# A decoder layer on one core: background work moved between scores and values, key differences that last a whole unit, and the row of maxima turned by VectorE and DRAM

## The chip, the cores and the metric

The kernel runs on 1 core of one Trainium2 chip. The metric is device time in microseconds, the median of several runs; before the change it is 2693.47 us (three runs, 2692.97 to 2693.5). A profile is one execution taken by the hardware profiler, with times in microseconds (us) unless marked ns. Engines are named as in it: PE is TensorE's matmul, PEld its weight load, DVE is VectorE, ACT ScalarE, POOL GpSimd, SP SyncE, which here issues every DMA.

## What is computed

Two sequences of 2048 tokens with 512 features go through one layer, all in float32:

```python
x = x + attn(layernorm(x), W_q, W_k, W_v, W_o)   # 16 heads of 32, rotary positions, full softmax
x = x + xattn(layernorm(x), ctx, ctx)            # gelu(x @ ctx.T) @ ctx, 77 rows of context
x = x + ffn(layernorm(x), weights, scale, bias)  # clip((x @ sign(weights).T) * scale + bias, -100, 100)
```

The softmax of the attention is taken with the maximum subtracted: `exp((q.k - max) / sqrt(32))`, divided by its sum over all 2048 keys.

## The kernel before

**Stages.** For each of the two batches, `project_batch` makes queries, keys and values chunk by chunk (128 tokens each) and keeps them in SBUF: keys and queries transposed, features on partitions, so that the four heads of a group `g` lie on four quarters of 32 partitions. `Attention.run` then does the attention. What follows it for a block of 512 tokens (output projection, the attention on the context, the feed-forward) is the generator `after_attention`, which is put into `queue` and taken piece by piece as *background*. After the second batch a tail does the last block alone.

**Units, steps, halves.** A unit `u` is 256 queries of one group of four heads (32 units a batch). It has 8 steps `i` (`STEPS`), each with two chunks of keys for all four heads, done in two halves of two heads. In `run`, the loop over `heads, others` writes the order of PE, DVE, ACT and POOL by hand (`tc.manual_schedule`): PE gets scores of the two heads (L565), maxima of the other two for a later step (L472), more scores; ACT takes the exponentials (L705), POOL adds the two chunks (L707), DVE reduces the maxima (L484). Then come the values of the *previous* step (`weigh`, L583) and the sums of the step before that (`total`, L597), then background. SP's order is not written out by hand.

**Row of maxima.** Scores are formed with keys on partitions, so the maximum of a query must be subtracted along the free axis. `lower` (L550) does it by a matmul that starts a score bank with the negative maxima, from `mrow`. To get there, `maxima` computes scores with queries on partitions, `AHEAD` steps ahead of their use; `split_maxima` writes each maximum as three bfloat16 parts (POOL) into `mt`; `turn_maxima` turns that by one DMA transposition (L504), for unit 0 by PE (L508).

**Differences of keys.** The four score banks of a unit are not cleared at each step: step `i` adds the product with the *difference* of two key blocks (`dk`, built by `key_steps`), so a bank moves from one block of keys to the next. The steps go through the four key blocks twice, first their first halves, then their second halves. At steps 0 and 4 (`i % NB == 0`) the bank is begun anew: `lower`, and keys instead of differences.

**PSUM.** Score banks `st` are four buffers of pool `ps_t`. The maxima `ps` and, during attention, the outputs of background pieces share the three buffers of `ps_s` in turn, so a maxima matmul waits until DVE has reduced what was in its buffer.

**Background.** Each `yield` of `after_attention` ends a piece and says whether the next one has PE work (`True`: heavy). `background(n, light=True)` runs nothing if the next piece is heavy. A block's heavy pieces are four projections (`po`, L382), four turns kept (`pt`, L345), one product with the context (`ph`, L389), four products back (`po`, L408), and four times a turn (`pt`) and a product of the feed-forward (`pf`, L363): 21 in all. Before, a heavy piece may run behind the second half of any step; in the last four units behind the first half too.

**Division.** A unit's sums and values end in one bank `acc`; in the first steps of the next unit `divide` copies it (ACT L611), takes reciprocals in two parts (DVE L617) and multiplies (POOL L620), one part for each `finish()`. In step 1 of a unit there are no sums due, so `total` issues nothing.

**Lead-in.** The maxima of the first `AHEAD` steps of a batch are computed in `project_batch`: `open_block` makes a step due when its block of keys is complete, `att.lead` issues them between the projections. The last ones, with `split_maxima(0)` and `turn_maxima(0)`, are in an order written by hand at its end (L254 to L274).

Of the kernel before, what the change touches and what calls it, by code (L numbers as in the profile page):

```python
# [16 lines left out]
P = 128  # L17
# [8 lines left out]
HQ = 256  # L26
NU = NB * ND * 2
STEPS = NCH // 2
AHEAD = STEPS + 2
SCALE = 1.0 / math.sqrt(DK)  # L30
EPS = 1e-5
MAX_VAL = 100.0
# [4 lines left out]
def decoder_layer(  # L37
# [48 lines left out]

    x_next = [load_x(0, 0), load_x(0, 1)]
    qkv = load_qkv()
    cos = const.tile([P, NCH, DK // 2], F32, tag="cos", name="cos")
    sin = const.tile([P, NCH, DK // 2], F32, tag="sin", name="sin")  # L90
    nc.sync.dma_start(cos, rope_cos.rearrange("(p c) d -> p c d", p=P))
    nc.sync.dma_start(sin, rope_sin.rearrange("(p c) d -> p c d", p=P))

    ident = const.tile([P, P], F32, tag="ident", name="ident")
    make_identity(nc, ident)
# [7 lines left out]
    nc.scalar.activation(minus_half, ones[:, :CPB], AF.Identity, scale=-0.5)  # L103


    mts = []
    for n in range(2):
        mt = const.tile([P, 2, 4, DK], BF16, tag=f"mt{n}", name=f"mt{n}")
        nc.vector.memset(mt, 0.0)
        mts.append(mt)  # L110

    late = {}

# [63 lines left out]

    def project_batch(b, ahead, att, xnt, wk, wq, wv):  # L180
        def times(dst, xnt, w, part=range(ND)):
            for i in part:
                nc.tensor.matmul(dst, xnt[:, i, :], w[:, i, :], start=(i == 0), stop=(i == ND - 1))  # L183
# [22 lines left out]

        def rotate(ch, a, ps, r):
            half = [P, H, DK // 2]
            cs = cos[:, ch, None, :, None].to_broadcast(half + [2])
            sn = sin[:, ch, None, :].to_broadcast(half)  # L210
# [234 lines left out]
    class Attention:  # L445
# [13 lines left out]
        def maxima(self, n, heads):  # L459
# [25 lines left out]

            return reduce

        def split_maxima(self, u):
            mx = self.mx.pop(u)
            neg = small.tile([P, 2, 4], F32, tag="neg", name="neg")  # L490
            nc.vector.tensor_reduce(neg, mx, AX.X, ALU.max, negate=True)
            mt = mts[u % 2]
            nc.gpsimd.tensor_copy(mt[:, :, :, 0], neg)
            nc.gpsimd.tensor_tensor(neg, neg, mt[:, :, :, 0], ALU.subtract)
            nc.gpsimd.tensor_copy(mt[:, :, :, 1], neg)
            nc.gpsimd.tensor_tensor(neg, neg, mt[:, :, :, 1], ALU.subtract)
            nc.gpsimd.tensor_copy(mt[:, :, :, 2], neg)


        def turn_maxima(self, u):  # L500
            mt = mts[u % 2]
            mrow = small.tile([P, 2, P], BF16, tag="mrow", name="mrow")
            if u > 0:
                nc.sync.dma_start_transpose(mrow, mt.rearrange("p c h d -> p (c h d)"))  # L504
            else:
                pt = ps_s.tile([P, 2, P], BF16, tag="s", name="ptm")
                for c in range(2):
                    nc.tensor.transpose(  # L508
                        pt[:, c, :], mt[:, c].rearrange("p h d -> p (h d)"), ident_b
                    )  # L510
                nc.vector.tensor_copy(mrow, pt)
            self.mrow[u] = mrow.rearrange("p c q -> p (c q)")

        def key_steps(self):
            self.dk = [None] + [
                const.tile([P, ND, BLK], F32, tag=f"w{n}", name=f"dk{n}") for n in "kqv"
            ]

            def differences(g):
# [12 lines left out]
            for _ in differences(0):  # L534
                pass
            queue.append(others())


        @staticmethod
# [19 lines left out]
        def scores(self, u, i, heads, c):  # L559
            qb, g, hf = self.units[u]  # L560
            kb, kc = divmod(self.chunk(i, c), CPB)
            keys = self.dk[kb] if kb else self.k[kb]
            for h in heads:
                r = self.rows[h]
                nc.tensor.matmul(  # L565
                    self.st[h][:, c, :],
                    keys[r, g, kc * P : (kc + 1) * P],
                    self.q[qb][r, g, hf * HQ : (hf + 1) * HQ],
                    start=False,
                    stop=True,  # L570
                    skip_group_check=True,
                )
# [74 lines left out]
        def run(self):  # L647
# [37 lines left out]
            for t in range(NU * STEPS):  # L685
# [10 lines left out]
                pw = big.tile([P, 4, 2, HQ], F32, tag="s", name="pw")  # L696
                sm = sums.tile([P, 4, HQ], F32, tag="sm", name="sm")
                for heads, others in (((0, 1), (2, 3)), ((2, 3), (0, 1))):
                    if i % NB == 0:
                        self.lower(u, heads)  # L700
                    self.scores(u, i, heads, 0)
                    reduce = self.maxima(t + AHEAD, others)
                    self.scores(u, i, heads, 1)
                    for h in heads:
                        nc.scalar.activation(pw[:, h], self.st[h], AF.Exp, scale=SCALE)  # L705
                    hs = slice(heads[0], heads[1] + 1)
                    nc.gpsimd.tensor_add(sm[:, hs, :], pw[:, hs, 0, :], pw[:, hs, 1, :])  # L707
                    if reduce:
                        reduce()
                    if heads[0] == 0:  # L710
                        first_half()
                        finish()
                        if u >= NU - ND:
                            background(1)
                        elif t % 2 == 1:
                            background(1, light=True)
                    else:
                        finish()
                        second_half()
                        if prev is not None and prev[1] == STEPS - 1:  # L720
                            finish()
                        if (t + AHEAD) % STEPS == STEPS - 1 and u + 1 < NU:
                            self.split_maxima(u + 1)
                            self.turn_maxima(u + 1)
                        background(1)
                prev = (u, i, pw, sm)
            xnt = turn(xn) if more else None
            first_half()
# [8 lines left out]
    xnt = turn(norm(x_next, 0, 0, nc.vector))  # L737
    for b in range(B):
        att = Attention(b)
        project_batch(b, x_next, att, xnt, *qkv)  # L740
        if b == 0:
            late_loads()
        load_ctx(b)
# [1 line left out]
        if b + 1 < B:  # L745
            x_next = att.x_next
            qkv = load_qkv()
    alone.append(True)
    queue += tail
    while queue:  # L750
# [49 lines left out]
```

## Time and profile before

| | |
|---|---|
| median of three runs | 2693.47 us |
| the profiled execution's own time | 2693.15 us |
| its span, first to last instruction | 2691.0 us |
| mean granted TensorE clock | 0.998 of full speed |
| PE matmuls of L550 | 512, 385 ns each at the median |
| DVE reductions of maxima, L484 | 2048, 682 ns each, 1308.9 us busy |
| POOL additions, L707 | 1024, 1272 ns each, 1295.2 us busy |
| DMA transpositions of the row, L504 | 62, landing in the median 2.3 us after issue |
| first attention | starts near 212 us, the second near 1545 us |
| tail without attention | from 2643.66 us on |

A row of groups says: line, engine, operation, output and inputs by the program's names, shapes, count, then busy time, mean duration of one, and idle time of the engine just before, with what ended it. A float32 matmul is two instructions, so L472 counts 4096 for 2048 maxima. Matmuls are pipelined and their ends are modelled, so the time that a stretch of PE work costs is read from one start to the next, not from durations. In the timeline, equal neighbours are merged: start, length, engine, line, count.

### The profile page before, as it was taken

What the parts mean: (1) busy time and instruction counts of PE and PEld (TensorE: products, weight loads), DVE (VectorE), ACT (ScalarE), POOL (GpSimd) and SP (SyncE); (2) the same over time, 40 slices, a digit from 0 to 9 for tenths busy, and PEclk for the clock granted to TensorE, in tenths of its full rate; (3) what the DMA queues carried; (4) which work ended last, traced back from release to release, by engine and by line L of the source; (5) the groups of instructions that cost most, each with busy time, mean ns of one, the idle gap of its engine ahead of it and who ended that gap; (6) DMA issues with size and microseconds to landing.
All of it is one profiled execution on the core that took longest, in us unless ns stands there. A gap on an engine that the chain in (4) does not pass through costs nothing.

```text
span 2691.0 us, 70222 instructions
## 1 busy us (share of the span) xinstructions
PE 2668.3 (99%) x30756; PEld 1490.3 (55%) x30756; DVE 1710.0 (64%) x2863; ACT 1321.0 (49%) x2394; POOL 1732.8 (64%) x1876
## 2 busy tenths in 40 slices
PE   8999999999999999999999999999999999999998
PEld 4445555555555555555554455555565555555555
DVE  3447777676766766676344477766767667766754
ACT  2115555455546554555422155555555455546553
POOL 3227777567857785677543287766687567857772
PEclk9999999999999999999999999999999999999999
DMA  3010000000000000000201000000000000000000
GB/s 126 24 32 2 5 4 4 4 4 18 20 3 4 12 28 3 4 12 26 73 25 40 5 4 4 4 4 4 4 27 12 4 4 19 19 4 4 19 19 17
DMA packets 38019, 43.54 MB, mean 16 GB/s; under 512 B 20662, under 2 KB 20918, under 8 KB 37712
## 3 DMA queue, kind: packets, MB, share of 16 engines
q1 hardware_dynamic: 37712, 39.05, 4.8%
q8 instruction: 241, 3.95, 0.6%
q14 instruction: 66, 0.54, 0.1%
HBM read 26.58 MB, written 8.39 MB: 13 GB/s over the span
## 4 chain that ended last, share of the span: by engine, by line
PE 98%; DVE 1%; DMA 0%; issue 0%; ACT 0%; POOL 0%; SPq 0%; POOLq 0%; ACTq 0%
PE st L565 23%; PE acc L583 22%; PE ps L472 18%; PE acc L597 8%; PE po L382 4%; PE pk L183 4%; PE pq L183 4%; PE pv L183 4%; PE st L550 3%; PE pf L363 2%; PE pt L345 1%; PE po L408 1%; PE ptqk L191 1%; PE ph L389 1%; PE pt L173 1%; DMA wk<-in_wk_t_dram 0%
## 5 line engine op out<-in xcount | busy, mean ns | idle before, releaser
L707 POOL TENSOR_TENSOR sm<-pw 128x512 f32<-128x512 f32 x1024 | 1295.2, 1272 | 599.5 <-ACT pw L705 596.8
L484 DVE TENSOR_REDUCE mx<-ps 128x1 f32<-128x512 f32 x2048 | 1308.9, 682 | 513.0 <-PE ps L472 509.1
L705 ACT ACTIVATE pw<-st 128x512 f32<-128x512 f32 x2048 | 1111.4, 595 | 947.0 <-PE ps L472 619.4
L472 PE MATMUL ps<-k,q 32*128 32x512 f32 x4096 | 1187.8, 640 | 0.0
L583 PE MATMUL acc<-pw,v 128*32 128x256 f32 x8192 | 655.1, 391 | 0.0
L597 PE MATMUL acc<-sm,ones 128*32 128x128 f32 x7680 | 388.8, 280 | 0.0
L583 PEld LDWEIGHTS acc<-pw,v 128*32 128x32 f32 x8192 | 162.5, 108 | 396.6 <-issue 378.3
L472 PEld LDWEIGHTS ps<-k,q 32*128 32x128 f32 x4096 | 352.4, 183 | 20.2 <-issue 13.8
L597 PEld LDWEIGHTS acc<-sm,ones 128*32 128x32 f32 x7680 | 248.6, 110 | 153.2
L565 PE MATMUL st<-q,dkk 32*128 32x256 f32 x2048 | 291.2, 400 | 0.0
L565 PE MATMUL st<-q,dkq 32*128 32x256 f32 x2048 | 290.0, 400 | 0.0
L565 PE MATMUL st<-q,dkv 32*128 32x256 f32 x2048 | 290.0, 400 | 0.0
L565 PE MATMUL st<-q,k 32*128 32x256 f32 x2048 | 262.8, 375 | 0.0
L565 PEld LDWEIGHTS st<-q,dkk 32*128 32x128 f32 x2048 | 175.8, 184 | 89.5 <-issue 51.3
L565 PEld LDWEIGHTS st<-q,dkq 32*128 32x128 f32 x2048 | 173.0, 184 | 79.9 <-issue 54.1
L565 PEld LDWEIGHTS st<-q,dkv 32*128 32x128 f32 x2048 | 175.0, 184 | 58.6 <-issue 26.3
L565 PEld LDWEIGHTS st<-q,k 32*128 32x128 f32 x2048 | 195.4, 187 | 14.0
L219 POOL TENSOR_TENSOR r<-r 128x512 f32<-128x512 f32 x64 | 81.1, 1268 | 161.8 <-DVE r L218 151.5
L617 DVE RECIPROCAL num<-num 128x128 f32<-128x128 f32 x128 | 120.4, 942 | 53.5 <-ACT num L611 53.5
L137 DVE BATCH_NORM_STATS2 st<-x 128x6 f32<-128x512 f32 x96 | 65.4, 686 | 91.7 <-DMA x<-in_x_dram 91.4
L183 PE MATMUL pk<-wk,xnt 128*128 128x512 f32 x256 | 118.2, 606 | 2.4 <-ACT xnt L175 1.3
L382 PE MATMUL po<-wo,q 128*128 128x512 f32 x256 | 117.4, 603 | 0.0
(109 smaller groups left out, 1784.9 us busy)
## 6 DMA issues: line engine op xcount, KB each, us to landing
x<-in_x_dram SPq DMA_DIRECT2D x64, 256.0 KB, 2.8
out_dram<-x SPq DMA_DIRECT2D x32, 256.0 KB, 2.0
wk<-in_wk_t_dram SPq DMA_DIRECT2D x2, 1024.0 KB, 7.8
wq<-in_wq_t_dram SPq DMA_DIRECT2D x2, 1024.0 KB, 9.9
wv<-in_wv_t_dram SPq DMA_DIRECT2D x2, 1024.0 KB, 5.5
wo<-in_wo_t_dram SPq DMA_DIRECT2D x1, 1024.0 KB, 9.9
wf<-in_wf_t_dram SPq DMA_DIRECT2D x1, 1024.0 KB, 5.0
mrow<-mt SPq DMA_TRANSPOSE x62, 2.3
```

The lines of the kernel that those rows point to most:

```text
L183: nc.tensor.matmul(dst, xnt[:, i, :], w[:, i, :], start=(i == 0), stop=(i == ND - 1))
L219: nc.gpsimd.tensor_add(r[:, 0, a], r[:, 0, a], r[:, 1, a])
L382: nc.tensor.matmul(ps, ot[:, i, cols], wo[:, i, :], start=(i == 0), stop=(i == ND - 1))
L472: nc.tensor.matmul(ps, self.q[qb][self.rows[h], g, q0 : q0 + P], self.k[kb][self.rows[h], g, :], start=True, stop=True,)
L484: nc.vector.tensor_reduce(mx[:, qc, h, kb : kb + 1], ps, AX.X, ALU.max)
L550: nc.tensor.matmul(self.st[h], ones_b[r, :], mrow[r, None, :].to_broadcast([DK, 2, HQ]), start=True, stop=False, skip_group_check=True,)
L565: nc.tensor.matmul(self.st[h][:, c, :], keys[r, g, kc * P : (kc + 1) * P], self.q[qb][r, g, hf * HQ : (hf + 1) * HQ], start=False, stop=Tr ...
L583: nc.tensor.matmul(acc[self.rows[h], 0, :], self.v[self.chunk(i, c)][:, d0 : d0 + DK], pw[:, h, c, :], start=(i == 0 and c == 0), stop=(i ...
L597: nc.tensor.matmul(acc[self.rows[h], 1, part], ones, sm[:, h, part], start=False, stop=(i == STEPS - 1), skip_group_check=True,)
L617: nc.vector.reciprocal(num[:, 1, part], num[:, 1, part])
L705: nc.scalar.activation(pw[:, h], self.st[h], AF.Exp, scale=SCALE)
L707: nc.gpsimd.tensor_add(sm[:, hs, :], pw[:, hs, 0, :], pw[:, hs, 1, :])
```

## The change

`lower` runs at step 0 only. Step 4 goes on from step 3 by one more difference, `wrap`, from the first half of the last key block to the second half of the first; POOL makes it when the group changes. `AHEAD` becomes `STEPS + 3`. The row of maxima is turned in another way: the parts are laid out as 128x32, DVE transposes the four 32x32 squares, SP stores the result to DRAM and reads it back by eight small DMAs into `mrow`; this is queued one step after the split. Background moves from behind the sums to between scores and values. In units 0 to 23, heavy pieces run only in the first half of step 1 and the second halves of steps 3 and 6; light ones keep to odd first halves and to second halves. The tables of angles leave their permanent place and are loaded into a buffer of `sums` for each batch.

```diff
-AHEAD = STEPS + 2
+AHEAD = STEPS + 3
...
+    def load_angles():
+        angles = sums.tile([P, 2, NCH, DK // 2], F32, tag="sm", name="angles")
+        for n, table in enumerate((rope_cos, rope_sin)):
+            nc.sync.dma_start(angles[:, n], table.rearrange("(p c) d -> p c d", p=P))
+        return angles
...
+    first_mt = zeros([P, 2, 4, DK], "first_mt")
+    mts = [zeros([P, 4, DK // 4], f"mt{n}") for n in range(2)]
+    mrows = [zeros([P, 2, P], f"mrow{n}") for n in range(2)]
...
         def split_maxima(self, u):
...
+                by_head = mts[u % 2][:, :, 0:6].rearrange("p h (c n) -> p c h n", n=3)
+                parts = [by_head[:, :, :, n] for n in range(3)]
+            for n in range(3):
+                if n:
+                    nc.gpsimd.tensor_tensor(neg, neg, parts[n - 1], ALU.subtract)
+                nc.gpsimd.tensor_copy(parts[n], neg)
...
-                nc.sync.dma_start_transpose(mrow, mt.rearrange("p c h d -> p (c h d)"))
...
+                square = small.tile([P, DK], BF16, tag="square", name="square")
+                nc.vector.transpose(square, mts[u % 2].rearrange("p h n -> p (h n)"))
+                rows = dram.tile([P, DK], BF16, tag="rows", name="rows")
+                nc.sync.dma_start(rows, square)
+                by_row = rows.rearrange("(a h n) i -> n a h i", a=4, h=4)
+                for h in range(4):
+                    for c in range(2):
+                        nc.sync.dma_start(
+                            mrow[h * DK : h * DK + 3, c].rearrange("n (a i) -> n a i", a=4),
+                            by_row[3 * c : 3 * c + 3, :, h, :],
+                        )
...
+        def wrap_around(self, g):
+            if self.wrap is None or self.wrap[0] != g:
+                d = small.tile([P, BLK // 2], F32, tag="wrap", name="wrap")
+                nc.gpsimd.tensor_sub(
+                    d, self.k[0][:, g, BLK // 2 :], self.k[NB - 1][:, g, : BLK // 2]
+                )
+                self.wrap = g, d
...
-            keys = self.dk[kb] if kb else self.k[kb]
+            if i == NB:
+                keys = self.wrap[1][:, None, :].to_broadcast([P, ND, BLK // 2])
+                kc = c
+            else:
+                keys = self.dk[kb] if kb else self.k[kb]
...
-                    if i % NB == 0:
+                    if i == 0:
                         self.lower(u, heads)
+                        self.wrap_around(self.units[u][1])
...
-                    if heads[0] == 0:
-                        first_half()
-                        finish()
-                        if u >= NU - ND:
+                    paced = u < NU - 2 * ND
+                    first = heads[0] == 0
+                    light = paced and (i, first) not in ((1, True), (3, False), (6, False))
+                    if first:
+                        if i == 1 or u >= NU - ND:
                             background(1)
                         elif t % 2 == 1:
                             background(1, light=True)
+                        first_half()
+                        finish()
                     else:
+                        background(1, light=light or i == 0)
                         finish()
                         second_half()
                         if prev is not None and prev[1] == STEPS - 1:
                             finish()
+                        if (t + AHEAD) % STEPS == 0 and u + 1 < NU:
+                            self.turn_maxima(u + 1)
                         if (t + AHEAD) % STEPS == STEPS - 1 and u + 1 < NU:
                             self.split_maxima(u + 1)
-                            self.turn_maxima(u + 1)
-                        background(1)
```

More of the change, by code (lines that the diff above doesn't have):

```diff
@@ L88, in decoder_layer @@
     qkv = load_qkv()
[L89 to L92, printed above, removed]
+    def load_angles():
[3 more added lines that the diff above has]
+        return angles
+    angles = load_angles()
     ident = const.tile([P, P], F32, tag="ident", name="ident")
@@ L103, in decoder_layer, with zeros @@
     nc.scalar.activation(minus_half, ones[:, :CPB], AF.Identity, scale=-0.5)
[L106 to L110, printed above, removed]
+    def zeros(shape, name):
+        t = const.tile(shape, BF16, tag=name, name=name)
+        nc.vector.memset(t, 0.0)
+        return t
+    first_mt = zeros([P, 2, 4, DK], "first_mt")
+    mts = [zeros([P, 4, DK // 4], f"mt{n}") for n in range(2)]
+    mrows = [zeros([P, 2, P], f"mrow{n}") for n in range(2)]
+    dram = ctx.enter_context(tc.tile_pool(name="dram", bufs=2, space=bass.MemoryType.DRAM))
     late = {}
@@ L176, in turn, with project_batch @@
         return xnt
-    def project_batch(b, ahead, att, xnt, wk, wq, wv):
+    def project_batch(b, ahead, att, xnt, angles, wk, wq, wv):
         def times(dst, xnt, w, part=range(ND)):
@@ L208, in rotate @@
             half = [P, H, DK // 2]
-            cs = cos[:, ch, None, :, None].to_broadcast(half + [2])
-            sn = sin[:, ch, None, :].to_broadcast(half)
+            cs = angles[:, 0, ch, None, :, None].to_broadcast(half + [2])
+            sn = angles[:, 1, ch, None, :].to_broadcast(half)
             pairs = ps.rearrange("p (h i t) -> p h i t", i=DK // 2, t=2)
@@ L491, in split_maxima @@
             nc.vector.tensor_reduce(neg, mx, AX.X, ALU.max, negate=True)
[L492 to L497, printed above, removed]
-        def turn_maxima(self, u):
-            mt = mts[u % 2]
-            mrow = small.tile([P, 2, P], BF16, tag="mrow", name="mrow")
-            if u > 0:
-                nc.sync.dma_start_transpose(mrow, mt.rearrange("p c h d -> p (c h d)"))
-            else:
+            if u == 0:
+                parts = [first_mt[:, :, :, n] for n in range(3)]
+            else:
[5 more added lines that the diff above has]
+                nc.gpsimd.tensor_copy(parts[n], neg)
+        def turn_maxima(self, u):
+            mrow = mrows[u % 2]
+            if u == 0:
                 pt = ps_s.tile([P, 2, P], BF16, tag="s", name="ptm")
@@ L508, in turn_maxima @@
                     nc.tensor.transpose(
-                        pt[:, c, :], mt[:, c].rearrange("p h d -> p (h d)"), ident_b
+                        pt[:, c, :], first_mt[:, c].rearrange("p h d -> p (h d)"), ident_b
                     )
                 nc.vector.tensor_copy(mrow, pt)
+            else:
+                square = small.tile([P, DK], BF16, tag="square", name="square")
[9 more added lines that the diff above has]
+                        )
             self.mrow[u] = mrow.rearrange("p c q -> p (c q)")
@@ L519, in key_steps @@
             ]
+            self.wrap = None
             def differences(g):
@@ L561, in scores @@
             kb, kc = divmod(self.chunk(i, c), CPB)
-            keys = self.dk[kb] if kb else self.k[kb]
+            if i == NB:
+                keys = self.wrap[1][:, None, :].to_broadcast([P, ND, BLK // 2])
+                kc = c
+            else:
+                keys = self.dk[kb] if kb else self.k[kb]
             for h in heads:
@@ L739, in decoder_layer @@
         att = Attention(b)
-        project_batch(b, x_next, att, xnt, *qkv)
+        project_batch(b, x_next, att, xnt, angles, *qkv)
         if b == 0:
@@ L747, in decoder_layer @@
             qkv = load_qkv()
+            angles = load_angles()
     alone.append(True)
```

## The prediction, before the changed kernel was run

> **What bounds the kernel now.** I read the page first: busy shares, then the chain of waits.
>
> ```profile
> PE 2668.3 (99%) x30756; PEld 1490.3 (55%) x30756; DVE 1710.0 (64%) x2863; ACT 1321.0 (49%) x2394; POOL 1732.8 (64%) x1876
> ...
> PE 98%; DVE 1%; DMA 0%; issue 0%; ACT 0%; POOL 0%; SPq 0%; POOLq 0%; ACTq 0%
> ```
>
> TensorE sets the end, but its busy time is a union of pipelined matmuls and hides stalls inside a stretch. So I went to the timeline and took start-to-start times. Names: S is a score stretch (L565 beside the maxima L472, with L550 where the row of maxima is written), V the values (L583), T the totals (L597), B a background piece. Half ia is step i's half with scores of heads 0 and 1, half ib the other. The view by stretches gives a whole unit without background:
>
> ```profile
> 241.82:272.91 31.09, 31.09 (x452) 18.00 (x449) 22.22 (x36) 17.95 (x34) 25.68 (x27) 1.00 0.02 4
> ```
>
> (stretch; length, then PE, PEld, DVE, ACT, POOL busy). The timeline of the next unit, halves 1a to 2b, shows where TensorE waits:
>
> ```profile
> 278.35 0.64 PE L583 MATMUL acc<-pw,v 128*32 128x256 f32 x8
> 278.46 1.29 DVE L484 TENSOR_REDUCE mx<-ps 128x1 f32<-128x512 f32 x2 [1.11 <-PE ps L472]
> ...
> 278.92 0.49 PE L565 MATMUL st<-q,dkk 32*128 32x256 f32 x2
> ...
> 279.66 0.94 DVE L617 RECIPROCAL num<-num 128x128 f32<-128x128 f32 x1
> ...
> 280.25 0.64 PE L583 MATMUL acc<-pw,v 128*32 128x256 f32 x8
> ...
> 280.52 1.22 DVE L484 TENSOR_REDUCE mx<-ps 128x1 f32<-128x512 f32 x2
> ...
> 280.82 0.48 PE L565 MATMUL st<-q,dkq 32*128 32x256 f32 x2
> ...
> 281.20 0.69 PE L472 MATMUL ps<-k,q 32*128 32x512 f32 x1
> ...
> 281.66 0.94 DVE L617 RECIPROCAL num<-num 128x128 f32<-128x128 f32 x1
> ...
> 282.25 0.64 PE L583 MATMUL acc<-pw,v 128*32 128x256 f32 x8
> ```
>
> An unhindered S lasts 1.07 us (277.28 to 278.35). S of 1b takes 1.33 (278.92 to 280.25), S of 2a 1.43 (280.82 to 282.25): the second maxima matmul waits for a score bank that DVE has not reduced (three banks, two per half), and DVE is also doing the two reciprocals of the division. It happens here because half 1a and 1b have no T: V to S is 0.57, where V, T to S is 0.79. Start-to-start times of all whole units give these stalls: 1b 0.26, 2a 0.36, 2b 0.14, and 0.04 in each later b-half but 4b. A long B behind 1b's V clears 2a and most of 2b. So DVE sets some 55 us (0.86 a unit on average, 64 units), matmul throughput the rest.
>
> Last, what a change of work costs TensorE:
>
> ```profile
> 606.06 0.64 PE L583 MATMUL acc<-pw,v 128*32 128x256 f32 x8
> ...
> 606.51 0.40 PE L597 MATMUL acc<-sm,ones 128*32 128x128 f32 x8
> 606.85 0.30 PEld L408 LDWEIGHTS po<-ctx,u 77*128 77x128 f32 x2 [0.20 <-DVE mx L484]
> 606.85 1.13 PE L408 MATMUL po<-ctx,u 77*128 77x512 f32 x2
> ...
> 607.90 0.39 PE L550 MATMUL st<-mrow,ones_b 32*128 32x512 bf16 x2
> ```
>
> V to T costs only V's streaming (0.46). T lasts 0.33 whether S or B follows, with 0.21 of streaming: 0.12 of switch. L408 streams 0.85 and takes 1.05: 0.20 for its first weight load and the switch out.
>
> **The change, part by part.**
>
> *Unit-long differences.* Row L550 goes in step 4, both halves: an S with L550 lasts 1.18, without 1.07, so 2 x 0.11 x 64 units = **-14.1 us**. Less than L550's 3% of the chain: its matmuls run on two row groups while the maxima fill the other two. What is late next is the bank: 4b falls back to the usual 0.04 (+2.6, counted below). The wrap difference is 40 POOL subtractions of 128x256 (0.46 for 128x128, 1.27 for 128x512: about 0.7) and POOL is idle 36% of the span; first read four steps later: 0, at most 1 us if that cover failed.
>
> *AHEAD 10 to 11.* Inside attention the maxima ride beside the scores: S without L472 at the end is 1.06. So a step dropped there saves nothing, and one more in the lead-in costs. Its four matmuls now come directly behind another group, and wait bank by bank for four reductions (2.48 us at 1540.02 in the second batch): the values at 1539.93 start near 1543.05, +3.1, less 0.3 that L508 waits for POOL today; +2.8 in the first batch. **+5.6 us** (2.2 if no bank were waited for, 7 if all reductions are).
>
> *Background moved from behind T to between S and V.* Switches: T-B-S against T-S, and S-B-V against S-V. The unknown is B to V. Nearest by what both touch is V to T: all 128 rows, no gap, T's weights loaded under V. Nearest by size of array is V to B: in 1b, V followed by L382 lasts 0.57, against 0.46 before T: 0.11 of drain. The Trainium skill, TensorEngine Tiling (Array Packing), Key Properties, says that changing the tiling mode, not just the tile, drains TensorE; 128x128 to 128x32 is such a change. By that rule S-B-V costs what T-B-S costs: **0**. By the row V to T, 0.12 is saved for each of 63 + 74 pieces: -16.5. I take the drain; the trace's V to B has the same pair of modes.
>
> *Which pieces, where.* Following the loop, a block's 21 TensorE pieces fill exactly 1a, 3b, 6b of seven units. The piece at 1a removes the stall of 1b if it is longer than about 0.9, but what is behind it on DVE moves into the short halves 1a to 2b. For a projection piece (L382 or L408, then the addition 0.69) the next light piece, at 1b, is the statistics (0.69 + 0.18), ahead of the second reciprocal. From the end of S in 1b: reductions to 1.3, statistics to 2.1, reciprocal to 3.0, first reduction of 2a to 3.6; S of 2b wants that bank at 2.7: stall 0.95. With 0.26 in 2a, 1.22 (L382) or 1.28 (L408). By the same sums: a turn kept (0.59 long) 0.27 + 0.26 + 0.19 = 0.72; a turn of the feed-forward, whose "low" waits for ACT behind two exps and holds up the first reciprocal, 1.47; L363 0.46; none 0.76. Test of the method: in before, a feed-forward turn at 1b must give 0.38 in 2a, and the timeline has 0.37. Over both batches: 6 x 1.22 + 10 x 1.28 + 8 x 0.72 + 8 x 0.46 + 4 x 1.47 + 20 x 0.76 + 2.0 for six mixed units = 52.7 us; before, 62 x 0.65 = 40.3. **+12.4**. Elsewhere: 4b +2.6, statistics at 4b 14 x 0.11 = +1.5, short turns +0.8, today's statistics at 2b and 7b -2.3: **+2.6**. Bounds: -11 if pieces at 1a only cover (below), +20 if each delay also reaches 3a.
>
> *Rows of maxima.* The split is queued one step earlier, so POOL's five casts (1.4 us) end before DVE's transposition at the end of 5b; the transposition has no row, lies between 0.1 and 0.3 (the 128x32 reduction L491 is 0.19; I take 0.15), and the half has 0.5 us spare on DVE: 0. Behind it on DVE wait the reductions of 6a; if POOL came 1 us late, TensorE would wait 0.5. Then SP issues a store and eight reads.
>
> ```profile
> x<-in_x_dram SPq DMA_DIRECT2D x64, 256.0 KB, 2.8
> out_dram<-x SPq DMA_DIRECT2D x32, 256.0 KB, 2.0
> ...
> mrow<-mt SPq DMA_TRANSPOSE x62, 2.3
> ```
>
> From the end of S in 5b: DVE done 1.5, store landed 3.5, reads issued every 0.44 (five loads took 2.23), the fourth landed 6.9 to 7.7, the eighth 8.7 to 9.5. Heads 0 and 1 need the first four at 0.79 + 4 x 1.87 = 8.3, heads 2 and 3 the rest at 10.2; a piece at 6b adds 0.6 to 3.6. **0**, down to 0.6 us of slack; stores of results wait on the same queue. The Trainium skill, VectorE: DVE Perf Modes, The three transpose paths, speaks against it: a strided plain copy is 19 times slower than the DMA transposition when the innermost destination stride is large, always use the latter. By it, 19 x 2.3 = 44 us, 35 too late in each of 62 units, +2,200 us (an estimate). I keep the rows: the squares are turned by DVE and each run is 32 contiguous values.
>
> *Small ones.* Angles reload behind the weights at 1326 and are first needed when the first key projection ends, near 1332.5: 0, +1 if not. Memsets: 0.
>
> **Sum:** -14.1 + 5.6 + 12.4 + 2.6 = +6.5 on the profiled execution's 2693.15 (span 2691.0 and 2.15 around it), 2699.6; the runs' median, 2693.47, is 0.3 above it: **2700 us**.
>
> **Rivals.** (1) *B to V needs no drain*: -16.5 more, 2683; for it V to T, against it V to B and the rule. It decides (faster by over 0.2%) from 0.09 a piece. (2) *The piece at 1a is plain cover*: 41 units lose 0.26 at 1b (-10.7), 12 lose the relief of 2a (+5.5), nothing piles up: -14.1 + 5.6 - 5.2 + 2.6 = -11, 2682. For it: B clears stalls in before; against it, DVE is ordered and its 4.4 us in 1b and 2a exceed those halves. (3) *Rows late*: slower; each microsecond beyond the slack in the units without a piece at 6b (about 18) is 18 us, in all 62 of them 62; 2718 to 2760. It needs store plus read above 5.4 us.
>
> **Numbers.** Forecast 0.52 (own range 2694 to 2707), (1) 0.10, (2) 0.22, (3) 0.10, more pile-up on DVE 0.06. Range 2683 to 2711, which leaves out most of (3) and half of (1). 0.2% (5.4 us) is about what can be told from no change. Faster 0.24: (1), and 0.14 of (2). Same 0.25: 0.17 of the forecast, 0.08 of (2). Slower 0.51.
>
> **What would show it.** L550 x256; S of 4a at 1.07, 4b at 1.11; S of 2b near 2.0 in units with a projection piece at 1a; V behind B starting 0.09 after B's streaming; mrow never waited for. I am wrong if S-B-V is cheaper than T-B-S, or if 2b doesn't stall.

## The result, and the profile after

The changed kernel takes **2708.14 us** (median of four runs, 2707.93 to 2710.06), the kernel before 2693.22 beside it: a ratio of 1.0057, 95% interval 1.004 to 1.0075. That is slower, by about 15 us where the prediction's sum had 6.5. Its range, 2683 to 2711, holds the time; its likeliest case's own range, 2694 to 2707, just misses it. The profiled execution took 2710.06 us, with a span of 2708.3 against 2691.0. It is the slowest of the four, so the profile has 17.3 us to account for where the medians have 15.

The page after: first the busy shares, then the chain of waits by engine.

```profile
PE 2675.3 (99%) x30500; PEld 1478.2 (55%) x30500; DVE 1718.0 (63%) x2925; ACT 1317.5 (49%) x2394; POOL 1761.3 (65%) x1919
...
PE 96%; ACT 1%; POOL 1%; DVE 1%; DMA 1%; issue 0%; SPq 0%; POOLq 0%; ACTq 0%
```

TensorE still sets the end and has 256 instructions fewer: the starts of the sums in step 4 are gone. But its share of the chain falls from 98% to 96%. Of the others only DVE had 1%; now three engines and the DMAs have 1% each. So the new time is waits for work that ends on other engines.

The view by stretches of two units (stretch; length, then PE, PEld, DVE, ACT, POOL busy; clock, DMA share, GB/s):

```profile
275.56:306.47 30.91, 30.91 (x448) 17.78 (x445) 22.35 (x37) 17.99 (x34) 26.42 (x27) 1.00 0.01 3
708.80:745.41 36.61, 35.13 (x464) 20.09 (x461) 25.06 (x40) 20.67 (x38) 30.60 (x30) 1.00 0.10 31
```

A whole unit without background takes 30.91 us instead of 31.09. The 0.18 is two starts of sums (0.22) less the 0.04 that half 4b now waits. Unit 15, below it, is not filled by TensorE: 36.61 us with 35.13 busy. Its end, in the timeline (start, length, engine, line):

```profile
737.14 1.92 POOL L387 TENSOR_SCALAR y<-y 128x512 f32<-128x512 f32 x1
...
739.14 1.27 POOL L388 TENSOR_TENSOR x<-x,y 128x512 f32<-128x512 f32 x1
...
740.44 0.34 SPq L389 DMA_DIRECT2D out_dram<-x  x1
...
740.87 0.38 SPq L528 DMA_DIRECT2D rows<-square  x1
...
742.48 0.33 SPq L75 DMA_DIRECT2D x<-in_x_dram  x1
...
742.91 2.54 SPq L532 DMA_DIRECT2D mrow<-rows  x8
...
743.57 0.40 PE L635 MATMUL acc<-sm,ones 128*32 128x128 f32 x8
...
745.41 0.09 PEld L584 LDWEIGHTS <-ones_b 32*128 32x128 bf16 x1 [1.71 <-DMA mrow<-rows]
745.41 0.81 PE L584 MATMUL st<-mrow,ones_b 32*128 32x512 bf16 x2 [1.44 <-DMA mrow<-rows]
```

From the totals (743.57) to the next scores (745.41) are 1.84 us, where 0.33 is usual. The start of the sums (L584) waits for the row of maxima. The row was ready on VectorE at 736.2, but SyncE's queue was held by the store of a result chunk (L389), which waited for GpSimd's clamp and addition (L387, L388) until 740.44. Then the load of a chunk of the next block (L75) waited for that store to land, and only behind it came the eight reads. SyncE's own waits in this stretch (waits in us, times, longest):

```profile
SPq L389 <- POOL x L388: 23.4, 1, 23.4
SPq L75 <- DMA out_dram<-x: 1.1, 1, 1.1
```

The store ahead is the larger part. It holds the row's own store back by 4.7 us. The reads then start 2.04 us behind the row's store; where nothing stands between the two, as in 55 of this run's 62 rows, they start 1.47 us behind it at the median, so the load adds about 0.6. The view of waits, summed over the span (waits in us, times, longest), has new lines; before, waits for `mrow` from a DMA came to 0.2 us:

```profile
PEld L584 <- DMA mrow<-rows: 8.6, 8, 2.8
...
PE st L584 <- DMA mrow<-rows: 6.4, 4, 2.5
...
PEld acc L635 <- POOL sm L746: 2.4, 8, 0.3
```

The third line is totals that wait for GpSimd's sums (L746), which come late behind the clamp and the addition.

The other new loss is the one foretold. Half 2a to 3a of unit 17, with an output projection at 1a:

```profile
797.91 0.69 DVE L149 BATCH_NORM_STATS2 st<-x 128x6 f32<-128x512 f32 x1
...
798.63 0.18 DVE L150 BATCH_NORM_AGGREGATE stats<-st 128x2 f32<-128x6 f32 x1
...
798.73 0.92 DVE L655 RECIPROCAL num<-num 128x128 f32<-128x128 f32 x1
799.29 0.48 PE L603 MATMUL st<-q,dkq 32*128 32x256 f32 x2
...
799.57 2.54 DVE L496 TENSOR_REDUCE mx<-ps 128x1 f32<-128x512 f32 x4
...
800.25 0.18 PEld L484 LDWEIGHTS ps<-k,q 32*128 32x128 f32 x1 [0.65 <-DVE mx L496]
...
801.30 0.64 PE L621 MATMUL acc<-pw,v 128*32 128x256 f32 x8
```

The statistics (L149, L150) stand ahead of the second reciprocal, four reductions come in a row behind it, and the second maxima matmul of 2b waits for a bank. S of 2b runs from 799.29 to 801.30: 2.01 us, where 1.07 is unhindered.

### The profile page after: what moved, and what is told of

It is laid out like the page before. It is cut to its first block, busy times and chain, and to the rows that moved or that the text cites. A ratio compares the mean times of both kernels' runs of the same rounds, so it can differ in the third digit from the quotient of the medians.

```text
span 2708.3 us, 70749 instructions
## 1 busy us (share of the span) xinstructions
PE 2675.3 (99%) x30500; PEld 1478.2 (55%) x30500; DVE 1718.0 (63%) x2925; ACT 1317.5 (49%) x2394; POOL 1761.3 (65%) x1919
## 4 chain that ended last, share of the span: by engine, by line
PE 96%; ACT 1%; POOL 1%; DVE 1%; DMA 1%; issue 0%; SPq 0%; POOLq 0%; ACTq 0%
PE st L603 23%; PE acc L621 21%; PE ps L484 18%; PE acc L635 8%; PE po L394 4%; PE pk L195 4%; PE pq L195 4%; PE pv L195 4%; PE pf L375 2%; PE st L584 2%; PE pt L357 1%; PE po L420 1%; PE ptqk L203 1%; PE ph L401 1%; ACT pw L744 1%; PE pt L185 1%
## 5 line engine op out<-in xcount | busy, mean ns | idle before, releaser
L746 POOL TENSOR_TENSOR sm<-pw 128x512 f32<-128x512 f32 x1024 | 1296.8, 1272 | 583.9 <-ACT pw L744 578.4
L603 PE MATMUL st<-q,wrap 32*128 32x256 f32 x1024 | 144.9, 400 | 0.0
L603 PE MATMUL st<-q,k 32*128 32x256 f32 x1024 | 133.5, 377 | 0.0
L149 DVE BATCH_NORM_STATS2 st<-x 128x6 f32<-128x512 f32 x96 | 65.4, 686 | 92.1 <-DMA x<-in_x_dram 91.8
```

What stands on the lines that cost most here:

```text
L149: nc.vector.bn_stats(st, xc)
L603: nc.tensor.matmul(self.st[h][:, c, :], keys[r, g, kc * P : (kc + 1) * P], self.q[qb][r, g, hf * HQ : (hf + 1) * HQ], start=False, stop=Tr ...
```

## The experiments

Every kernel ran beside the kernel before, whose median there was 2692.5 to 2692.8. "Waits of S" are start-to-start times of score stretches above the unhindered 1.07 us (1.18 with the start of the sums), added up over the 60 whole units 1 to 30 of each batch in the profiled executions.

### One part after another

**Differences alone.** The kernel before with `wrap_around`, `if i == 0` for `lower`, and the angles per batch:

```diff
-            keys = self.dk[kb] if kb else self.k[kb]
+            if i == NB:
+                keys = self.wrap[1][:, None, :].to_broadcast([P, ND, BLK // 2])
+                kc = c
+            else:
+                keys = self.dk[kb] if kb else self.k[kb]
...
-                    if i % NB == 0:
+                    if i == 0:
                         self.lower(u, heads)
+                        self.wrap_around(self.units[u][1])
```

> Kept of the change: the unit-long differences (each wrap-around difference is made once per pair of heads' queries, not twice per unit) with the angles loaded per batch. Undone: the new path of the maxima's rows and its earlier start, and the placement of the background pieces. My theory, from the prediction's sum with those terms taken out: -14.1 for the differences, +2.6 for what then stalls at half 4b, so about 2682 (2679 to 2686). Rival A, the differences were never on the path (POOL is not what ends a wait at 4a and 4b): within 2 us of the before kernel's 2693. Rival B, the relief only moves the wait to the next half: between, about 2688.

Measured: 2682.19 us, ratio 0.9961 (0.9949 to 0.9974): 10.5 us less than the kernel before. The sums' starts were on the path, and half 4b falls back as worked (3.5 us of waits, from 0.1). GpSimd makes the wrap-around difference only when the group changes, 40 times in all at 0.74 us, not once per pair of heads as written above. This part alone is an improvement.

**One step earlier, alone.** On top of it:

```diff
-AHEAD = STEPS + 2
+AHEAD = STEPS + 3
```

> The kernel of the first experiment (unit-long differences, the background and the transposing DMA of before) with the maxima one step further ahead, 11 steps instead of 10, and nothing else. bg_old, which has the new rows' path as well, took 12 us more than that kernel. My theory: the lead-in alone costs two times 2.8 = 5.6 us, and the other 6 are of the new path (the square at half 5b, 0.22 in 12 units, and rows late at 0a, about 0.5 in 8): 2688 (2686 to 2690). Rival A, all 12 us come with the earlier start: 2694. Rival B, the earlier start costs nothing by itself: 2682.

Measured: 2689.85 us, ratio 0.999 (0.9982 to 0.9999), +7.7 against the kernel without it. The first unit starts 2.4 us later (244.15 against 241.74), the stretch from batch 0's last unit to batch 1's first grows by 2.8. Together 5.2, close to the 5.6 of the theory. Inside the attention half 5b loses 3.3 us: in 12 units with output projections or products back its scores wait 0.43 us instead of 0.13. The split's reduction on VectorE (L501) has moved from the end of 5b to the end of 4b, where a piece's statistics (L146) stand as well. The timeline of such a unit:

```profile
484.39 0.19 DVE L501 TENSOR_REDUCE neg<-mx 128x8 f32<-128x32 f32 x1
484.50 0.69 DVE L146 BATCH_NORM_STATS2 st<-x 128x6 f32<-128x512 f32 x1
...
485.32 1.25 DVE L493 TENSOR_REDUCE mx<-ps 128x1 f32<-128x512 f32 x2
```

So the reductions of 5a begin 1.59 us after its scores (483.73); without the earlier step it was 1.30. The 0.29 between them is what 5b waits longer.

**With the new path of the rows.** The changed kernel with the placement of before:

```diff
-                    if first:
-                        if i == 1 or u >= NU - ND:
+                    if heads[0] == 0:
+                        first_half()
+                        finish()
+                        if u >= NU - ND:
                             background(1)
                         elif t % 2 == 1:
                             background(1, light=True)
-                        first_half()
-                        finish()
                     else:
-                        background(1, light=light or i == 0)
...
+                        background(1)
```

> The changed kernel with one part undone: background pieces stand after the totals as before, at most one light and one at will per step. The new rows' path and its earlier start stay. My theory: what the new placement costs is about 20 us (12.4 as predicted for the pile-up of DVE work at 1a to 2b, 9 for the rows that come late behind a result's store in units 15 and 23, which depends on where the store's piece falls), so about 2682 plus 5.6 for the two longer lead-ins = 2688 (2685 to 2692). Rival A, late rows belong to the new path whatever the placement: 2688 + 9 = 2697. Rival B, the placement costs nothing and the loss is in the rows' path: 2706 to 2709.

Measured: 2694.23 us, ratio 1.0005 (0.9997 to 1.0014), another +4.4. Rival A had the right idea and twice the size. The row is late here too, at 0a of eight units, 0.34 to 0.73 us each (4.0 us). SyncE's timeline:

```profile
671.99 0.32 SPq L528 DMA_DIRECT2D rows<-square  x1
677.02 0.34 SPq L389 DMA_DIRECT2D out_dram<-x  x1
677.47 2.52 SPq L532 DMA_DIRECT2D mrow<-rows  x8
```

The row is stored at once, but its reads stand behind a result's store, which waited for GpSimd: 5.5 us from the row's store to the first read, with no load between. With nine instructions in two groups, the path can be cut in the middle.

**Old path, new placement.** The opposite pair:

```diff
-AHEAD = STEPS + 3
+AHEAD = STEPS + 2
...
-                square = small.tile([P, DK], BF16, tag="square", name="square")
-                nc.vector.transpose(square, mts[u % 2].rearrange("p h n -> p (h n)"))
...
+            if u > 0:
+                nc.sync.dma_start_transpose(mrow, mt.rearrange("p c h d -> p (c h d)"))
```

> The changed kernel with the other part undone: the maxima's rows are turned by the transposing DMA as before and started one step later (lead-in of 10 steps again). The new placement and the unit-long differences stay. My theory: 5.6 us come back with the lead-ins, and the 9 us of rows late behind a result's store mostly go too, since the one transposing DMA needs one issue where the new path needs nine after a landing: about 2694 (2692 to 2699). Rival A, the rows would wait behind the store whatever path they take, since they are on the same queue: 2708 - 5.6 = 2702.5. Rival B, the new path is what costs, all of it: below 2690.

Measured: 2698.52 us, ratio 1.0021 (1.0013 to 1.003). The placement alone costs 16.3 us against the first experiment, more than the whole change loses. The row is late with the single transposing DMA as well: in the waits of this kernel,

```profile
PEld L570 <- DMA mrow<-mt: 9.1, 8, 1.8
```

and on SyncE the transposition stands behind the same two instructions:

```profile
734.80 0.34 SPq L386 DMA_DIRECT2D out_dram<-x  x1
737.45 0.34 SPq L75 DMA_DIRECT2D x<-in_x_dram  x1
737.89 1.17 SPq L514 DMA_TRANSPOSE mrow<-mt  x1
```

So in this placement the row is late on either path: it is the slot of the last piece that does it. My theory that the single DMA escapes was wrong. Its range, 2692 to 2699, holds the time, but not for its reason: the rows cost 7.5 us here, where it had them mostly gone.

| kernel | median us | step |
|---|---|---|
| before | 2692.7 | |
| differences | 2682.2 | -10.5 |
| + one step earlier | 2689.9 | +7.7 |
| + new path of the rows | 2694.2 | +4.4 |
| + new placement (the change) | 2708.1 | +13.9 |

### What in the placement costs

**Behind the totals, in the same halves.**

```diff
                     if first:
+                        first_half()
+                        finish()
                         if i == 1 or u >= NU - ND:
                             background(1)
                         elif t % 2 == 1:
                             background(1, light=True)
-                        first_half()
-                        finish()
```

and likewise at the end of the second halves.

> The changed kernel with its pieces in the same halves of a unit, but each behind the totals, as in the kernel before, not between scores and values. My theory: a piece costs the same in either place (both have one change of the array's tiling in and one out), and the loss comes from the halves that were chosen, so 2708 again (2705 to 2711). Rival A, a piece between scores and values costs one more drain of the array: about 190 pieces of 0.09 us, 17 us less, 2691. Rival B, a piece behind the totals holds up the next scores and with them ScalarE's exponentials: 5 us more, 2713.

Measured: 2706.62 us, ratio 1.0051 (1.0038 to 1.0063): not to be told from the change. A projection piece takes 3.63 us from start to next start in either place. The place between scores and values is worth nothing either way; the halves are what counts.

**No light piece at 1b.**

```diff
-                        background(1, light=light or i == 0)
+                        if not paced or i != 1:
+                            background(1, light=light or i == 0)
```

> The changed kernel without the light piece at half 1b in the paced units, so that no normalisation's sums are made on VectorE between the two reciprocals; a piece that would have run there runs at the next place for it. My theory: the wait of the scores at 2b in the units with a projection piece at 1a falls from 0.94 us to 0.14, in 16 units about 13 us: 2695 (2692 to 2699). Rival A, the same work stalls the half it moves to by as much: 2706 to 2709. Rival B, the longer chain of pieces ends later and spills into the next projection: above 2709.

Measured: 2697.89 us (2695.56 to 2701.73), ratio 1.0021 (1.0013 to 1.0029): 10 us back. The waits of S at 2b fall from 20.4 to 10.1 us (the profile is of the slowest of these executions). A piece's statistics no longer stand between the reciprocals; in the units below 24 with a projection or a product back at 1a, 2b waits 0.14 us instead of 0.94, as the theory had it. The pile-up is VectorE's.

**Reciprocals in quarters.** On the first experiment's kernel, and then on the whole change:

```diff
-            for c in range(2):
-                part = slice(c * P, (c + 1) * P)
+            n = HQ // 4
+            for c in range(4):
+                part = slice(c * n, (c + 1) * n)
...
```

> The kernel of the first experiment with the reciprocals of a unit's totals cut from two of 128 columns into four of 64, one in each of the halves 1a, 1b, 2a and 2b. It tests whether the waits of the scores at 1b, 2a and 2b (0.26, 0.36 and 0.14 us in nearly every unit) are VectorE's pile-up: a half has about 0.58 us of VectorE left beside its two reductions of 0.68 us, and one reciprocal of 128 columns takes 0.94. My theory: a quarter takes about 0.5 us and fits, so 0.76 us go in most of 62 units, about 2637 (2633 to 2648). Rival A, VectorE has no time left over the four halves together, and half of the loss stays: about 2660. Rival B, the waits are of something else, such as ScalarE's copy of the totals: 2682.

> The changed kernel, whole, with only the reciprocals cut into four of 64 columns as in the run called quarters. If the 14 to 16 us that the new placement costs were for the larger part VectorE's pile-up of two long reciprocals, the projection's addition and the sums of a normalisation at 1a to 2b, the waits of the scores at 2a and 2b (16.6 and 20.4 us in 60 units) should all but go: about 2676 (2672 to 2682), and the distance to the run quarters, 2668, should shrink from the 26 us between the changed kernel and wrap_only to about 9 plus the 12 of the rows' path, less what the pieces at 1a save at 1b (6). Rival A, the sums and the addition alone still stall 2b by about 0.4 us in 16 units and more behind it: 2688. Rival B, they are not VectorE's: 2706.

Measured: 2667.73 us on the first (ratio 0.9907, 0.9893 to 0.992) and 2688.82 on the change (0.9986, 0.9979 to 0.9992), 14.5 and 19.3 us less. Waits of S, in us over 60 units:

| half | before | differences | change | quarters | quarters on the change |
|---|---|---|---|---|---|
| 1b | 15.2 | 15.2 | 9.4 | 15.2 | 11.6 |
| 2a | 17.3 | 17.3 | 16.6 | 0.4 | 7.5 |
| 2b | 6.0 | 6.0 | 20.4 | 2.1 | 7.8 |
| 3b | 3.2 | 3.2 | 3.6 | 8.1 | 3.5 |
| 4b | 0.1 | 3.5 | 2.3 | 3.3 | 2.2 |
| 5b | 2.6 | 3.3 | 5.6 | 3.1 | 5.1 |

The waits at 2a and 2b are the reciprocals'. The one at 1b is not: it stays at 0.26 us a unit. The timeline of quarters shows why:

```profile
710.03 1.29 DVE L493 TENSOR_REDUCE mx<-ps 128x1 f32<-128x512 f32 x2 [1.11 <-PE ps L481]
...
710.50 0.48 PE L589 MATMUL st<-q,dkk 32*128 32x256 f32 x2
...
711.23 0.54 DVE L642 RECIPROCAL num<-num 128x64 f32<-128x64 f32 x1
```

VectorE had been idle 1.11 us when the maxima of 1a came, and yet the scores of 1b, from 710.50, wait: 1a has no totals and lasts 1.64 us (708.86 to 710.50) instead of 1.9, which is less than matmul, two reductions and the next matmul need through three banks. The reciprocal comes later. In the prediction I had put 1b to the reciprocals too. A quarter costs 0.54 us, not half of 0.94, and in 12 units with an output projection or a product back at 1b the fourth comes just ahead of a piece's statistics:

```profile
511.44 0.54 DVE L642 RECIPROCAL num<-num 128x64 f32<-128x64 f32 x1
511.90 0.64 DVE L146 BATCH_NORM_STATS2 st<-x 128x6 f32<-128x512 f32 x1
...
512.67 2.61 DVE L493 TENSOR_REDUCE mx<-ps 128x1 f32<-128x512 f32 x4
```

There 3b waits 0.54 us instead of 0.13 (5 us given back). The theory also counted 0.76 us in most of 62 units, 45 us, where the three rows of the table hold 38.5. Of these 15.2 stay at 1b and 2.5 at 2a and 2b; less the 5 at 3b, some 16 were to be had, and 14.5 came. On the change, Rival A held: the projection's addition and the statistics still stall 2b by 0.54.

**A piece at 1a, with care.** On quarters:

```diff
+                        if i == 1 or u >= NU - ND:
+                            background(1)
+                        elif i in (5, 7):
+                            background(1, light=True)
...
-                        background(1)
+                        if u >= NU - ND or i not in (1, 2):
+                            background(1)
```

> The run quarters with one thing taken from the change and placed with care: pieces of any weight at half 1a, which has no totals and is 0.3 us shorter than the others, so that the scores at 1b wait 0.26 us in it, and no piece at 1b, 2a, 2b and 3a, where the quarters of the reciprocals run on VectorE. My theory: with a piece at 1a the wait at 1b goes in some 25 units (6 us), and the 8 us of waits at 3b (the fourth quarter beside a piece's VectorE work) mostly too: 2656 (2653 to 2660). Rival A, fewer places push pieces into the next projection, where they cost the same: 2660 to 2668. Rival B, the chain of pieces gets late enough to leave a longer end: above 2668.

Measured: 2668.06 us, ratio 0.9909 (0.9895 to 0.9922), the same as quarters. The expected gain came and went: 1b falls from 15.2 to 11.9 and 3b from 8.1 to 1.6, but 2a rises from 0.4 to 5.2, and at 0b of six units the totals wait for GpSimd's sums (6.1 us). In the timeline of one of them a clamp and an addition stand just ahead of these sums. The 6 us expected at 1b were too many as well: 3.3 came, and a piece at 1a shifts part of the wait to 2a. Quarters, the simpler of the two, beats both kernels by 25 and 40 us.

### What makes the rows late

**The result's store held back.** The store goes into a list at step 5 and is issued when step 6 begins, and SyncE's order is written by hand:

```diff
+                    mybir.EngineType.SP,
...
-            nc.sync.dma_start(tokens(out[b], blk * CPB + first + c), xs[c])
+            stores.append((tokens(out[b], blk * CPB + first + c), xs[c]))
+            if alone or not attending or attending[-1] != 5:
+                store()
...
+                if i == 6:
+                    store()
```

> The changed kernel, with the store of a finished result chunk held back on SyncE's queue from step 5 to the start of step 6 of the unit, and SyncE's instructions kept in the order they are written in, so that the maxima's rows are stored and read back before that store. Nothing else is moved. My theory: the waits of the sums' start for the rows of the maxima at half 7b of units 15 and 23 go, and with them their tail in 0a: 8 to 10 us of the two batches, about 2699 (2697 to 2702). Rival A, the rows are late because POOL and DVE finish the split late there, not because of the store ahead: 2706 to 2709. Rival B, the store that is held holds up the loads behind it (the next block's chunks), so the gain is lost there: 2703 to 2708, with new waits for x.

Measured: 2702.68 us, ratio 1.0037 (1.0025 to 1.005), 5.5 less than the change. SyncE in the same unit:

```profile
735.88 0.34 SPq L536 DMA_DIRECT2D rows<-square  x1
738.83 2.54 SPq L540 DMA_DIRECT2D mrow<-rows  x8
741.46 0.36 SPq L434 DMA_DIRECT2D out_dram<-x  x1
```

The reads begin 4.1 us sooner (738.83 against 742.91), and the waits at 7b, 0a and 0b, 9.6 us in all, are gone. But the order by hand also keeps the loads of the next block behind: in the next unit all four are issued from 763.50, and the addition that needs one starts at 766.28, though its product was done at 764.0. Half 4b of the four units behind the late rows now waits 1.0 to 1.15 us each, 4.1 us more than in the change: part of the gain went as Rival B said.

**The store on GpSimd's own queue.**

```diff
-            nc.sync.dma_start(tokens(out[b], blk * CPB + first + c), xs[c])
+            nc.gpsimd.dma_start(tokens(out[b], blk * CPB + first + c), xs[c])
```

> The changed kernel with the stores of the finished result chunks issued by GpSimd, which makes the values they store, and not by SyncE. No order is changed on another engine by hand. In bg_old and in the changed kernel the reads of the rows stood on SyncE behind such a store, which waited up to 4.6 us for GpSimd's clamp and addition. My theory: the rows are then stored and read as soon as they are made, the waits at 7b of units 15 and 23 (6.7 us), and at 0a and 0b behind them (3) go, and unlike in store_held no load of x is held: 2698 (2696 to 2700). Rival A, an issue on GpSimd takes about as long as one of its additions, 1.3 us, and the head sums behind it come late 32 times: up to 10 us given back, 2708. Rival B, rows are late because GpSimd splits the maxima late: 2707.

Measured: 2713.66 us, ratio 1.0077 (1.0064 to 1.0089). The theory failed, and the timeline of SyncE says how:

```profile
735.22 0.34 SPq L528 DMA_DIRECT2D rows<-square  x1
742.11 0.33 SPq L75 DMA_DIRECT2D x<-in_x_dram  x1
742.55 2.54 SPq L532 DMA_DIRECT2D mrow<-rows  x8
```

The row is stored 5.6 us sooner, and its reads stand where they stood, behind the load of the next block's chunk. That waits for the buffer, which means for the landing of the store, whichever queue issued it. The issue on GpSimd takes 0.63 us of that engine, and totals at 7a wait 4 us more than in the change.

**A fifth buffer for the chunks.**

```diff
-    xlate = ctx.enter_context(tc.tile_pool(name="xlate", bufs=4))
+    xlate = ctx.enter_context(tc.tile_pool(name="xlate", bufs=5))
...
-                d = small.tile([P, BLK // 2], F32, tag="wrap", name="wrap")
+                d = small.tile([P, BLK // 2], F32, tag="wrap", name="wrap", bufs=1)
```

> The changed kernel with a fifth buffer for the result chunks (four before), so that the load of a chunk of the next block no longer waits for the landing of the store just issued; the order of SyncE's instructions at the late rows stays: a result's store, the rows' store, the chunk's load, the rows' reads. Room is made by one buffer for the wrap-around difference instead of two, and by a temporary tile for the first unit's split maxima. store_pool took the store from that queue and the rows were as late as ever, behind the chunk's load, so my theory of the store alone has fallen. New theory: the load's wait, 1.2 us behind the store's landing, is what makes the rows late at 7b of units 15 and 23 (1.3 to 2.6 us there), and without it the reads end about 1.6 us sooner: 5 to 8 us less, 2701 (2699 to 2704). Rival A, the store's own wait for GpSimd is enough to make them late by as much: 2706 to 2709. Rival B, the load is late for other reasons and the reads start where they did: 2708.

Measured: 2708.58 us, ratio 1.006 (1.0046 to 1.0073): no change, and no test either.

```profile
739.85 0.34 SPq L389 DMA_DIRECT2D out_dram<-x  x1
740.28 0.38 SPq L529 DMA_DIRECT2D rows<-square  x1
741.89 0.33 SPq L75 DMA_DIRECT2D x<-in_x_dram  x1
742.33 2.53 SPq L533 DMA_DIRECT2D mrow<-rows  x8
```

The extra buffer let every load come forward by one: the load at this place is now that of the chunk after, and it waits for the same store. So the theory of the load stands untested by this run. Over all the runs, either of the two is enough to make the rows late: a result's store alone stood between the row's store and its reads in the old placement (5.5 us), a load alone with the store on GpSimd (7.3 us), and with neither, in the held store, no row was waited for. In the change itself both stand there, and the load adds only about 0.6 us to what the store has cost.

## Why the prediction was right, and what it missed

**The sign and the main terms held.** Against the sum of the prediction, with what the runs or the trace gave:

| term of the sum | predicted | measured |
|---|---|---|
| differences, with 4b | -11.5 | -10.5 (run) |
| one step earlier | +5.6 | +7.7 (run), of it about 5.2 in the lead-ins |
| path of the rows | 0 | +4.4 (run) |
| pile-up at 1b to 2b | +12.4 | +7.9 (trace, 60 units) |
| rest of the placement | 0 | +6 (the run's 13.9 less the 7.9) |

**Right for the stated reason.** The background's move as such costs nothing: 3.63 us in both orders, and the run with the pieces behind the totals is the same. That is what the drain gives, which I took from the rule. So Rival 1, no drain from B to V, is out. The streaming times in that part, 0.85 and 0.21 us, agree with the profile before, where projections (L183) start an instruction of 512 columns every 0.43 us: 0.86 for the two of a float32 product, 0.21 for 128 columns. Rival 2, plain cover, is out too: 2b stalls 0.94 in units with a projection at 1a, and S of 2b takes 2.01 where I wrote "near 2.0". L584 has 256 matmuls, and 4a and 4b behave as written.

**Mis-sized: the pile-up.** By kind of piece at 1a, the worked sums of the waits at 1b, 2a and 2b against the trace: output projection 1.22 and 1.20, product back 1.28 and 1.20, no piece 0.76 and 0.76, but a turn kept 0.72 and 0.40, a feed-forward turn 1.47 and 1.32, a feed-forward product 0.46 and 0.40. For a turn kept I carried a delay of 0.26 into 2a, and there is none. With the prediction's counts these differences are 0.1 + 0.8 + 2.6 + 0.6 + 0.5 = 4.6 us, by which 12.4 is too high. The sign owes something to this: with the pile-up at its measured size my sum would have been +2 us, no change to be told, and the rest of the 15 is waits that I had not priced.

**The step that failed: the rows of maxima, "0, down to 0.6 us of slack; stores of results wait on the same queue".** The last clause names the cause, and I priced it at nothing. The slack was worked out for a row that finds SyncE's queue free, and for such a row the steps were near: 0.20 us for the transposition (0.15 taken), 1.5 from the row's store to the first read (2.0), 0.32 from read to read (0.44). The 2,200 us of the copy 19 times slower, which I set aside, did not come either. But SyncE issues one after the other; a store in its queue waits for GpSimd, and a load behind the store waits for that store to land. In units 15 and 23, where the last feed-forward piece falls at 5a, the first read comes 6.7 us (once 7.9) after the row is ready on VectorE, and 1.5 us elsewhere at the median. In the change this is 6.7 us at 7b of units 15 and 23 of both batches and 2.9 at 0a and 0b behind them; in the run with the old placement, 4.0 at 0a. My Rival 3 said that rows would be late, but from another cause (store plus read too slow, in units without a piece at 6b), and so with the wrong place and two to six times the price: the rows' own store and reads are in time when nothing stands ahead of them. "mrow never waited for", one of the signs that I had named, did not hold.

**Also missed:** totals that wait for GpSimd behind the clamp (about 2.9 us more than before), and the wait at 5b that comes with the earlier split (3.0 us). With the rows' 9.6 these are 15.5; less the pile-up's 4.5, and less 1.9 at 4b, where I had 4.1 and the trace has 2.2, they leave 9 us and make 15.6 of the sum's 6.5. The medians have 15, the profiled execution, from which the waits are read, 17.3. Its own account closes: in the 60 whole units the waits of S are 16.1 us more and the starts of sums 13.2 less, totals wait 9.6 more, and what is left is 4.8, where the longer lead-ins took 5.2 when they were changed alone.

## What to carry to other kernels

Price a moved step on every in-order queue that it is put in, with what stands *ahead of* it there: a DMA that waits for a slow producer, or for a buffer, holds up all behind it, and another buffer may only bring the next such wait forward. A change made of several parts is best taken apart on the chip: here one part gains 10 us and the rest gives back 26. And where an engine has a little time left in each stretch, cut its long instructions to fit that time: two reciprocals made four gained 14.5 us, more than the change's one good part.

## What the runs showed of the hardware

The 32x32 transposition of a 128x32 bfloat16 tile on VectorE takes 0.20 us. With nothing between them on the queue, the row's way through DRAM, from the store's issue to the last read's issue, takes 4.0 us at the median and 3.9 to 6.2 over the 62 rows of the run with the held store; each of the eight reads holds SyncE for about 0.27 us, the transposing DMA for 1.17 us in one piece. A 256 KB store issued by GpSimd takes 0.63 us of that engine, against 0.34 on SyncE. A reciprocal of 64 columns takes 0.54 us and one of 128 takes 0.94, so, if the rest goes with the length, about 0.14 us of each do not (an estimate: twice 0.54 less 0.94).
